# A four-layer convolution net on one core: eight table copies of 64 lags, coefficient arrays loaded once on partition quarters, an unpadded intermediate, and earlier first Toeplitz loads

## The chip, the core and the metric

The kernel runs on one core of a Trainium2 chip, in float32. A core has TensorE (PE; its weight loads are shown as PEld), VectorE (DVE), ScalarE (ACT), GpSimd (POOL) and SyncE (SP), which work side by side, each through its own instructions in order. Transfers between HBM and the on-chip memory run on 16 DMA engines, which SP, ACT and POOL start. The metric is the device time of one execution in microseconds; the median of the runs counts.

## The reference

Four residual layers act on x of shape (8, 56, 56, 192), each behind a group norm. The change lies in layers 0 and 1, which are alike (576 channels inside, Toeplitz products along w and along h):

```python
rpe_input = [0, 1..55, 0, -1..-55]                 # 111 different lags are used
p = silu(x @ p_w.T + p_b)
q = silu(x @ q_w.T + q_b)
v = silu(x @ v_w.T + v_b)
sl = 0.95 + 0.05 * clip(slope, 0, 1)
decay = [1, sl**1..sl**55, 1, sl**55..sl**1]
a1 = mlp1(rpe_input) * decay                       # 1 -> 32 -> 32 -> 32 -> 32 -> 576
a2 = mlp2(rpe_input) * decay
qv = q * v
o1 = toeplitz(qv along w, a1)                      # per channel, 56 x 56
o2 = toeplitz(qv along h, a2)
out = (p * (o1 + o2)) @ o_w.T + o_b
x = x + out
```

Layer 2 is a 7 x 7 depthwise convolution with a two-layer network behind it, layer 3 windowed attention. They are not touched.

## The kernel before, in words

**Statistics.** `input_stats` reads the images in pairs (j = 0 to 3), in seven tiles each, through a buffer of 7 tiles, and takes batch statistics on DVE (L218). They feed the group norm (matmuls at L79).

**q and v.** `tno_qv` works on 2 image pairs at once, in groups of 256 tokens (loads at L240, normalised by ACT at L246), against 1152 columns of `wq` (matmuls L263, added to the bias by DVE at L272). The first two groups are done apart, one image pair at a time (`half_unit`, matmuls L284, additions L291), since only the first pair's statistics are there. ACT applies silu (L301), POOL multiplies q by v (L304), and SP stores the product to HBM as `qv` (L307). There `qv` is [18][64 * 56][128]: 18 blocks of 32 channels by 4 images; a block has 56 image rows of 56 pixels, and 8 rows of padding, which POOL fills with zeros by one transfer for each of the two `qv` arrays (L743).

**Coefficients.** `decay_tables` runs once for each of the two layers. It loads the slopes in five pieces (L145), makes the powers on DVE (L146 to L158), loads the small arrays of each coefficient network (L165 to L174), runs it on PE (L180, L187) and writes the coefficients times the decay (L194) to an HBM table (L204): for each 32 channels 16 rows, row g with the 60 lags from 4g on. Its buffers for the coefficients (`a`) turn over with two.

**Toeplitz.** `tno_toeplitz` walks 9 blocks of 64 channels, for each direction d = 0 (along w) and 1 (along h), 18 steps n in all. Each step loads `q`, 128 partitions of which 2 x 56 are used (d = 0 at L380 by two transfers, d = 1 at L383 by one), and `tm`, the coefficients shifted by one lag per partition, by four transfers (L393); both two steps ahead, through two buffers. PE multiplies (L406), ACT copies out (L413), DVE turns (L424), POOL adds (L429) and stores `L_sum`.

**Order.** `tno_layers` runs the first groups and the statistics by hand, then 28 rounds in which a unit of L263, a statistics tile and one step of each layer's coefficients follow each other, and then four Toeplitz stages, each woven by `weave` into other work of the layers (`tno_qv`, `tno_out`). `weave` counts nominal times that the generators yield; with `lo` the first Toeplitz step is due at 0.04 of the other work. A stage's first yield, after its first loads, counts 8. From the 28 rounds on, PE, DVE, ACT and POOL keep the order written; before them a scheduler places the instructions, as it does SP's throughout. SP's transfers are numbered over eight semaphores, so that each waits for the one eight places before it.

Of the kernel before, what the change touches and what calls it, by code (L numbers as in the profile page):

```python
# [12 lines left out]
F32 = mybir.dt.float32  # L13
# [25 lines left out]
def view(ap, offset, dims):  # L39

    return bass.AP(ap.tensor, ap.offset + offset, [ap.ap[0], *dims])


class Net:
# [86 lines left out]

    TG, TW = 16, 60

    def decay_tables(self, L, p, tables):

        nc, inp = self.nc, self.inp
        tv = p.tile([32, 111], F32, name=f"{L}tv", bufs=1)
        nc.sync.dma_start(tv, inp["tvec"])  # L140
        pows = []
        for c in range(5):
            m = min(128, D1 - 128 * c)
            sl = p.tile([128, 1], F32, name=f"{L}sl")
            nc.sync.dma_start(sl[:m], inp[f"{L}_slope"][128 * c : 128 * c + m, :])  # L145
            nc.vector.tensor_scalar(sl[:m], sl[:m], 0.0, 1.0, ALU.max, ALU.min)  # L146
            nc.vector.tensor_scalar(sl[:m], sl[:m], 1.0 - 0.95, 0.95, ALU.mult, ALU.add)
            pw = p.tile([128, 64], F32, name=f"{L}pw", bufs=5)
            nc.gpsimd.memset(pw[:m, 0:1], 1.0)
            n = 1  # L150
            while n < 64:
                nc.vector.tensor_scalar(
                    pw[:m, n : 2 * n], pw[:m, 0:n], sl[:m], None, ALU.mult
                )
                n *= 2
                if n < 64:
                    sq = p.tile([128, 1], F32, name=f"{L}sl")
                    nc.vector.tensor_mul(sq[:m], sl[:m], sl[:m])  # L158
                    sl = sq
            pows.append(pw)  # L160
            yield 1.0
        for d in range(2):
            t = f"{L}_t{d + 1}"
            w0 = p.tile([32, 2], F32, name="w0")
            nc.sync.dma_start(w0[:, 0:1], inp[f"{t}_w0"])  # L165
            nc.sync.dma_start(w0[:, 1:2], inp[f"{t}_b0"])
            ws = p.tile([32, 3, 32], F32, name="ws")
            nc.sync.dma_start(ws, inp[f"{t}_ws"])
            bs = p.tile([32, 3], F32, name="bs")
            nc.sync.dma_start(bs, inp[f"{t}_bs"])  # L170
            wo = p.tile([32, D1], F32, name="wo")
            nc.sync.dma_start(wo, inp[f"{t}_wo"])
            bo = p.tile([128, 5], F32, name="bo")
            nc.sync.dma_start(bo, inp[f"{t}_bo"])  # L174
            h = p.tile([32, 111], F32, name=f"{L}h")
            nc.vector.tensor_scalar(h, tv, w0[:, 0:1], w0[:, 1:2], ALU.mult, ALU.add)
            nc.vector.tensor_scalar(h, h, 0.0, None, ALU.max)
            for i in range(3):
                hp = self.bank2()[:32, 0, :111]
                nc.tensor.matmul(hp, ws[:, i, :], h, start=True, stop=True)  # L180
                h = p.tile([32, 111], F32, name=f"{L}h")
                nc.vector.tensor_scalar(h, hp, bs[:, i : i + 1], 0.0, ALU.add, ALU.max)
                yield 1.0
            for c in range(5):
                m = min(128, D1 - 128 * c)
                ap = self.bank2()[:, 0, :111]
                nc.tensor.matmul(  # L187
                    ap[:m], wo[:, 128 * c : 128 * c + m], h, start=True, stop=True
                )
                a = p.tile([128, 4 * self.TG + 56], F32, name=f"{L}a")  # L190
                nc.gpsimd.memset(a[:m, 111:], 0.0)
                back = view(pows[c][:m], 55, [[-1, 55]])
                for lo, hi, dec in ((0, 55, back), (55, 111, pows[c][:m, 0:56])):
                    nc.vector.scalar_tensor_tensor(  # L194
                        view(a[:m], 110 - lo, [[-1, hi - lo]]),
                        ap[:m, lo:hi],
                        bo[:m, c : c + 1],
                        dec,
                        ALU.add,
                        ALU.mult,  # L200
                    )
                for n in range(m // 32):
                    to = tables[d][self.TG * (4 * c + n) : self.TG * (4 * c + n + 1)]
                    nc.sync.dma_start(  # L204
                        to.rearrange("g (c w) -> c g w", w=self.TW),
                        view(a[32 * n : 32 * n + 32], 0, [[4, self.TG], [1, self.TW]]),
                    )
                yield 1.0

    def input_stats(self, xs, gn, j, p):  # L210

        nc = self.nc
        st = self.tp.tile([128, 3, 14, 6], F32, name="st", bufs=2)
        for t in range(NT):
            x = p.tile([128, 3, TT], F32, name="x", bufs=7)
            self.load_pair(x, xs, j, slice(t * TT, (t + 1) * TT))
            for k in range(3):
                nc.vector.bn_stats(st[:, k, t, :], x[:, k, :])  # L218
            yield
        self.norms.append(self.pair_gn_finish(st[:, :, :NT], gn, j))  # L220
        for more in self.all_norms():
            pass

    def tno_qv(self, L, j0, xs, gn, qv, apart=None, cols=(0, 2 * D1), g0=0):
# [72 lines left out]
        def multiply(m, n, z, at, c0):  # L297
            k = n // 128
            for f in stores:
                f()  # L300
            nc.scalar.activation(z[:m, :n, :], z[:m, :n, :], AF.Silu)  # L301
            prod = p.tile([128, 4, DC * 4], F32, name="t4")
            half = z[:m, :n, :].rearrange("p (n h c) b -> p n h (c b)", h=2, c=DC)
            nc.gpsimd.tensor_mul(prod[:m, :k], half[:, :, 0], half[:, :, 1])  # L304
            n0 = c0 // 128
            stores[:] = [
                lambda: nc.sync.dma_start(  # L307
                    qv[2 * n0 : 2 * n0 + 2 * k, at : at + m, :].rearrange("n t e -> t n e"),
                    prod[:m, :k].rearrange("p n (h e) -> p (n h) e", h=2),
                )  # L310
            ]
# [53 lines left out]
    def tno_toeplitz(self, j0, mats, qv, o):  # L365
# [6 lines left out]
        def load(n):  # L372
            blk, d = divmod(n, 2)
            q = p.tile([128, H, 128], F32, name="q", bufs=2)
            if d == 0:

                for half in range(2):
                    of = qv[2 * blk + half, :T].rearrange("(h w) e -> w h e", w=W)
                    by = nc.scalar if half and n > 1 else nc.sync
                    by.dma_start(q[64 * half : 64 * half + W], of)  # L380
            else:
                of = qv[2 * blk : 2 * blk + 2].rearrange("n (h w) e -> (n h) (w e)", w=W)
                nc.sync.dma_start(q.rearrange("p i e -> p (i e)"), of)  # L383
            return q

        def matrices(n):

            blk, d = divmod(n, 2)
            row = 32 * self.TW
            at = mats[d].offset + 2 * blk * self.TG * row  # L390
            for k in range(4):
                of = bass.AP(mats[d].tensor, at + k, [[row, 2 * self.TG], [1, row]])
                nc.sync.dma_start(self.tms[n % 2][k:128:4], of)  # L393

        def along(n, q, ot, g):
# [52 lines left out]
        for n in range(2):  # L448
            loaded.append(load(n))
            matrices(n)  # L450
        yield 8.0

        work = []

# [226 lines left out]
    def tno_layers(self, x0, x1, x2, gn, last):  # L681
# [11 lines left out]
        ]  # L693
        qvs = {

            j0: self.dram.tile([D1 // 32, 64 * W, 128], F32, name=f"qv{j0}") for j0 in (0, 2)
        }
        o = [self.dram.tile([B // 2, 9, 128, T], F32, name=f"{L}_sum") for L in LS]
        x = (x0, x1, x2)
        with ExitStack() as ctx, ExitStack() as wqp:  # L700
# [2 lines left out]
            Q = lambda i, j0, *more: self.tno_qv(LS[i], j0, x[i], gn[i], qvs[j0], *more)  # L703
            O = lambda i, j0, woven=True: self.tno_out(LS[i], j0, x[i], gn[i], o[i], x[i + 1], gn[i + 1], woven)
            TZ = lambda i, j0: self.tno_toeplitz(j0, tables[i], qvs[j0], o[i])
            QT, OT, TZT = 25 * 2.25 * 5.3, 28 * 10.7, 8 + 72 * 3.2

            with tc.tile_pool(name="tab", bufs=2) as tab:
                stats = [self.input_stats(x0, gn[0], j, tab) for j in range(4)]
# [1 line left out]
                    pass  # L711
                first, rest = Q(0, 0, tab, (0, 512)), Q(0, 0, None, (512, 2 * D1), 2)
                next(first)

                for n in range(14):
                    next(first)
# [10 lines left out]
                decay = [self.decay_tables(LS[i], tab, tables[i]) for i in range(2)]  # L727
                more = (dt for st in stats[2:] for dt in st)
                with tc.manual_schedule(engines=ENGINES):
                    for n in range(28):  # L730
# [8 lines left out]
                            next(decay[1])  # L739
                        if n in (14, 21):  # L740
                            qv = qvs[0 if n == 14 else 2]
                            to = qv[:, T:].rearrange("n (p k) e -> p n (k e)", p=112)
                            nc.gpsimd.dma_start(to, view(none, 0, [[0, D1 // 32], [1, 512]]))  # L743
                    for more in decay:
                        assert next(more, None) is None
                lanes = [[(rest, QT * 5 / 9 * 21 / 25 - 25.0), (Q(0, 2), QT)], [(O(0, 0), OT), (Q(1, 0), QT)]]
# [4 lines left out]
            with tc.tile_pool(name="tz", bufs=1) as self.tz, in_order:  # L751
# [928 lines left out]
```

## Time and profile before

| What | Value |
| --- | --- |
| Median of 3 runs | 5438.96 us (5432.41 to 5443.45) |
| The profiled execution | 5425.63 us |
| Its span | 5423.8 us |
| PE busy | 5166.0 us (95%) |
| DVE busy | 2589.3 us (48%) |
| ACT busy | 2383.5 us (44%) |
| POOL busy | 1767.2 us (33%) |
| Moved by DMA | 1116.48 MB, mean 206 GB/s |
| Granted TensorE clock, mean | 0.978 |

The span is the time from the first instruction to the last on the core. Busy times overlap, so they do not add up to the span. In the page's rows of 40 slices, each digit is a tenth of busy share in one fortieth of the span (135.6 us).

### The profile page before, as it was taken

To read this page: it belongs to the slowest core of one execution; us is meant where nothing else is said; L and a number is where in the kernel's file an instruction comes from. 1 tells how busy PE (TensorE), PEld (TensorE's weight loads), DVE (VectorE), ACT (ScalarE), POOL (GpSimd) and SP (SyncE) were. 2 spreads that over 40 slices of the span, in tenths; PEclk is the share of its full clock that TensorE was granted. 3 is DMA by queue.
4 is the path that set the end of the run, shared out by engine and by line. 5 is a ranking of instruction groups with operands and counts; after the bars stand their busy time and mean duration, and the time that the engine had idled before them with its cause. 6 is when DMAs were issued, how large, how long until landed. Compare 5 with 4: busy or idle time off the path is not lost.

```text
span 5423.8 us, 144350 instructions
## 1 busy us (share of the span) xinstructions
PE 5166.0 (95%) x64672; PEld 3811.2 (70%) x64672; DVE 2589.3 (48%) x3990; ACT 2383.5 (44%) x3179; POOL 1767.2 (33%) x1291
## 2 busy tenths in 40 slices
PE   7879999999999999999999899989999999999998
PEld 4657777777777777777777789856665444777776
DVE  6535556455555555555556422422222331566666
ACT  3345555444554454655455422243323333444443
POOL 2225675133664243546443100000000100333333
PEclk9889999999999999999999999999999999999998
DMA  7699997888786999889897667635454221445552
GB/s 251 151 243 283 289 311 234 265 281 267 241 262 176 307 317 318 279 226 291 285 312 266 205 223 248 229 96 190 135 174 124 75 68 49 85 98 108 101 102 68
DMA packets 1051146, 1116.48 MB, mean 206 GB/s; under 512 B 235200, under 2 KB 986304, under 8 KB 1036128
## 3 DMA queue, kind: packets, MB, share of 16 engines
q1 hardware_dynamic: 911584, 854.88, 52.9%
q0 software_dynamic: 38144, 200.99, 9.6%
q10 hardware_dynamic: 100800, 51.38, 3.9%
q8 instruction: 508, 8.32, 0.6%
q14 instruction: 110, 0.90, 0.1%
HBM read 743.17 MB, written 363.94 MB: 204 GB/s over the span
## 4 chain that ended last, share of the span: by engine, by line
PE 50%; DVE 3%; DMA 3%; issue 1%; ACT 1%; POOL 1%; SPq 0%; POOLq 0%; ACTq 0%; DVEq 0%
PE bank L980 7%; PE bank L837 5%; PE bank L1060 5%; PE bank L1254 4%; PE bank L263 4%; PE bank L592 3%; PE bank L1074 3%; PE bank L536 3%; PE bank L1370 2%; PE bank L1201 2%; PE bank L1284 2%; PE bank L1325 2%; PE bank L406 2%; PE bank L586 1%; PE bank L1344 1%
## 5 line engine op out<-in xcount | busy, mean ns | idle before, releaser
L263 PE MATMUL bank<-wq,t 128*128 128x256 f32 (+4 forms) x7680 | 1290.3, 374 | 72.1 <-DVE t L272 40.8
L263 PEld LDWEIGHTS bank<-wq,t 128*128 128x128 f32 (+2 forms) x7680 | 1005.2, 190 | 350.8 <-issue 92.4
L272 DVE TENSOR_TENSOR t<-bank,wq 128x1024 f32<-128x1024 f32 (+3 forms) x480 | 517.7, 1112 | 692.5 <-PE bank L263 537.1
L304 POOL TENSOR_TENSOR t<-t 128x1024 f32<-128x1024 f32 (+2 forms) x288 | 528.0, 1847 | 676.5 <-ACT t L301 339.1
L413 ACT COPY ot<-bank 128x896 f32<-128x896 f32 x576 | 493.4, 909 | 515.1 <-PE bank L406 401.8
L429 POOL TENSOR_TENSOR s<-s,ot 128x1568 f32<-128x1568 f32 x128 | 551.1, 4306 | 193.8 <-DVE ot L426 128.4
L301 ACT ACTIVATE t<-t 128x2048 f32<-128x2048 f32 (+2 forms) x288 | 423.0, 1488 | 328.8 <-DVE t L272 319.0
L406 PE MATMUL bank<-q,tm 56*32 56x224 f32 x18432 | 504.9, 353 | 22.0 <-DMA tm<-L_tab 10.6
L406 PEld LDWEIGHTS bank<-q,tm 56*32 56x32 f32 x18432 | 340.0, 106 | 148.2 <-issue 81.7
L122 POOL DMA_DIRECT2D x<-t x112 | 87.0, 777 | 1071.7 <-DVE t L601 1007.4
L560 DVE TENSOR_TENSOR t<-t,bank 128x896 f32<-128x896 f32 x224 | 242.8, 1088 | 401.6 <-ACT bank L555 346.0
L555 ACT ACTIVATE bank<-bank,wo 128x448 f32<-128x448 f32 x448 | 262.8, 605 | 377.4 <-PE bank L545 349.8
L980 PE MATMUL bank<-z,w 128*128 128x448 f32 (+1 forms) x1344 | 413.3, 555 | 2.8 <-DVE xt L828 2.8
L536 PE MATMUL bank<-t,wo 128*128 128x224 f32 x1792 | 375.9, 364 | 21.1 <-ACT t L515 10.6
L536 PEld LDWEIGHTS bank<-t,wo 128*128 128x128 f32 x1792 | 337.7, 194 | 51.7 <-issue 29.6
L592 PE MATMUL bank<-t,wo 128*128 128x224 f32 x1792 | 368.9, 359 | 0.0
L592 PEld LDWEIGHTS bank<-t,wo 128*128 128x128 f32 x1792 | 329.9, 190 | 31.1 <-issue 31.1
L980 PEld LDWEIGHTS bank<-z,w 128*128 128x128 f32 (+1 forms) x1344 | 183.0, 189 | 209.8 <-issue 199.5
L837 PEld LDWEIGHTS bank<-xt,cm 113*112 113x112 f32 x3072 | 309.7, 178 | 25.7 <-issue 23.3
L837 PE MATMUL bank<-xt,cm 113*112 113x108 f32 (+2 forms) x3072 | 316.0, 263 | 1.0 <-ACT h L989 1.0
L127 POOL DMA_DIRECT2D x<-x x64 | 36.7, 573 | 855.5 <-DVE x L1011 796.7
L424 DVE STREAM_TRANSPOSE s<-ot 128x1792 f32<-128x1792 f32 x144 | 292.8, 2034 | 24.5 <-ACT ot L413 16.2
(162 smaller groups left out, 6977.2 us busy)
## 6 DMA issues: line engine op xcount, KB each, us to landing
q<-qv SPq DMA_DIRECT2D x36, 3584.0 KB
t<-L_sum SPq DMA_DIRECT2D x112, 1008.0 KB
L_sum<-s POOLq DMA_DIRECT2D x256, 392.0 KB, 7.2
qv<-t SPq DMA_DIRECT2D x192, 512.0 KB
cm<-in_L_cm SPq DMA_DIRECT2D x96, 896.0 KB
tm<-L_tab SPq DMA_DIRECT2D x288, 240.0 KB
q<-qv SPq DMA_DIRECT2D x40, 1568.0 KB
q<-qv ACTq DMA_DIRECT2D x32, 1568.0 KB
```

The lines of the kernel that those rows point to most:

```text
L263: nc.tensor.matmul(pp[:m, b, 256 * j : 256 * j + k], x[rows, j, 2 if part else b, s : s + m], w[rows, part, c0 + c : c0 + c + k],  start=p ...
L272: nc.vector.tensor_add(z[:m, c : c + k, :], view(pp[:m], 0, [[1, k], [256, 4]]), view(bias[:m], c0 + c, [[1, k], [0, 4]]),)
L301: nc.scalar.activation(z[:m, :n, :], z[:m, :n, :], AF.Silu)
L304: nc.gpsimd.tensor_mul(prod[:m, :k], half[:, :, 0], half[:, :, 1])
L406: nc.tensor.matmul(pt[32 * j : 32 * j + 32, r, hf * 224 : (hf + 1) * 224], tm[rows, at : at + 32], q[rows, :, 4 * c : 4 * c + 4], start=Tr ...
L413: nc.scalar.copy(view(ot, 4 * (g % 4), [[16, 2], [32, 112], [1, 4]]), view(pt, 0, [[512, 2], [4, 112], [1, 4]]),)
L424: nc.vector.transpose(to, of.rearrange("p (i k) -> p i k", k=32))
L429: add.tensor_add(to, to, view(of, 0, [[1, 28], [32, 56]]))
L536: mm(gs[c // 2][:, b, c % 2 * 256 : c % 2 * 256 + N], pw[:, 0, 128 * c : 128 * c + 128], xn[:, b], start=c % 2 == 0, stop=False,)
L592: mm(P[:, b, :N], ow[:, c, 0:128], g[:, 4 * b + c], start=False, stop=c == 3)
L837: nc.tensor.matmul(pc[:, 128 * e + 4 * m0 : 128 * e + 4 * m1], cm[:113, e, k, :], xt[:, m0 - 1 + k : m1 - 1 + k, c + e, :], start=n == 0 a ...
L980: nc.tensor.matmul(phs[c][:, s, :TT], w0[rows, part, at : at + 128], z[rows, Z[2 if part else s], :], start=part == flip, stop=part != flip,)
```

## The change

Five edits come together.

1. The coefficient table keeps 8 rows of 64 lags for each 32 channels, row g with the lags from 8g on, instead of 16 rows of 60. A `tm` transfer reads each row twice, four lags apart.
2. The slopes (two transfers for each layer) and the arrays of all four networks are loaded at the start of `decay_tables`, which is now begun right after the first activation load. The four networks share five arrays, each on a quarter of the partitions. `a` has four buffers, and the statistics' tiles have six instead of seven.
3. `qv` has no padding within blocks: it is [18 * 56 * 56 + 448][128], and only the tail is filled with zeros. The d = 1 load of `q` still reads 64 rows for each half, of which the last 8 are the next block's and not used.
4. A Toeplitz stage's first yield counts 16 instead of 8.
5. In the first stage `lo` is 0.02 instead of 0.04.

The diff, cut to its core:

```diff
-    TG, TW = 16, 60
+    TG, TW = 8, 64
...
+        slopes = p.tile([128, 5], F32, name=f"{L}slopes", bufs=1)
+        nc.sync.dma_start(slopes[:, 0:4], of[:512, 0].rearrange("(c p) -> p c", p=128))
+        nc.sync.dma_start(slopes[:64, 4:5], of[512:D1, :])
+        nets = []
+        for d in range(2):
+            at = slice(64 * (L == "L1") + 32 * d, 64 * (L == "L1") + 32 * d + 32)
...
+            tv, w0, ws, bs, wo = net = [n[at] for n in self.nets]
+            nc.sync.dma_start(w0[:, 0:1], inp[f"{t}_w0"])
+            nc.sync.dma_start(w0[:, 1:2], inp[f"{t}_b0"])
+            nc.sync.dma_start(tv, inp["tvec"])
+            for to, n in ((ws, "ws"), (bs, "bs"), (wo, "wo"), (bo, "bo")):
+                nc.sync.dma_start(to, inp[f"{t}_{n}"])
+        yield 0.0
...
-                a = p.tile([128, 4 * self.TG + 56], F32, name=f"{L}a")
+                a = p.tile([128, 8 * self.TG + 56], F32, name=f"{L}a", bufs=4)
...
-                        view(a[32 * n : 32 * n + 32], 0, [[4, self.TG], [1, self.TW]]),
+                        view(a[32 * n : 32 * n + 32], 0, [[8, self.TG], [1, self.TW]]),
...
-            x = p.tile([128, 3, TT], F32, name="x", bufs=7)
+            x = p.tile([128, 3, TT], F32, name="x", bufs=6)
...
-                    qv[2 * n0 : 2 * n0 + 2 * k, at : at + m, :].rearrange("n t e -> t n e"),
+                    qv[2 * n0 * T : 2 * (n0 + k) * T].rearrange("(n t) e -> t n e", t=T)[at : at + m],
...
-                of = qv[2 * blk : 2 * blk + 2].rearrange("n (h w) e -> (n h) (w e)", w=W)
+                rows = qv.rearrange("(h w) e -> h (w e)", w=W)[2 * H * blk : 2 * H * blk + H + 64]
+                of = bass.AP(rows.tensor, rows.offset, [[H * W * 128, 2], [W * 128, 64], [1, W * 128]])
                 nc.sync.dma_start(q.rearrange("p i e -> p (i e)"), of)
...
-                of = bass.AP(mats[d].tensor, at + k, [[row, 2 * self.TG], [1, row]])
+                of = bass.AP(mats[d].tensor, at + k, [[row, 2 * self.TG], [4, 2], [1, row]])
...
-        yield 8.0
+        yield 16.0
...
-            j0: self.dram.tile([D1 // 32, 64 * W, 128], F32, name=f"qv{j0}") for j0 in (0, 2)
+            j0: self.dram.tile([D1 // 32 * T + 8 * W, 128], F32, name=f"qv{j0}") for j0 in (0, 2)
...
-            QT, OT, TZT = 25 * 2.25 * 5.3, 28 * 10.7, 8 + 72 * 3.2
+            QT, OT, TZT = 25 * 2.25 * 5.3, 28 * 10.7, 16 + 72 * 3.2
...
                 next(first)
+                decay = [self.decay_tables(LS[i], tab, tables[i]) for i in range(2)]
+                for more in decay:
+                    next(more)
...
-                            to = qv[:, T:].rearrange("n (p k) e -> p n (k e)", p=112)
-                            nc.gpsimd.dma_start(to, view(none, 0, [[0, D1 // 32], [1, 512]]))
+                            to = qv[D1 // 32 * T :].rearrange("(p k) e -> p (k e)", p=112)
+                            nc.gpsimd.dma_start(to, none)
...
-                    self.weave(lanes[n], tz, lanes[n + 1][0][0], TZT)
+                    self.weave(lanes[n], tz, lanes[n + 1][0][0], TZT, lo=0.04 if n else 0.02)
```

The matrices, the matmuls and every value computed stay the same.

More of the change, by code (lines that the diff above doesn't have):

```diff
@@ L128, in store_samples @@
             self.nc.gpsimd.dma_start(xs[j + 4 * s, 128:C, tok], of[HALF[s], 2, :])
-    TG, TW = 16, 60
+    TG, TW = 8, 64
     def decay_tables(self, L, p, tables):
         nc, inp = self.nc, self.inp
-        tv = p.tile([32, 111], F32, name=f"{L}tv", bufs=1)
-        nc.sync.dma_start(tv, inp["tvec"])
+        slopes = p.tile([128, 5], F32, name=f"{L}slopes", bufs=1)
+        of = inp[f"{L}_slope"]
+        nc.sync.dma_start(slopes[:, 0:4], of[:512, 0].rearrange("(c p) -> p c", p=128))
+        nc.sync.dma_start(slopes[:64, 4:5], of[512:D1, :])
+        nets = []
+        for d in range(2):
+            t = f"{L}_t{d + 1}"
+            at = slice(64 * (L == "L1") + 32 * d, 64 * (L == "L1") + 32 * d + 32)
+            if at.start == 0:
+                one = lambda n, shape: p.tile([128, *shape], F32, name=f"net{n}", bufs=1)
+                self.nets = one("t", [111]), one("w0", [2]), one("ws", [3, 32]), one("bs", [3]), one("wo", [D1])
+            bo = p.tile([128, 5], F32, name=f"{t}bo", bufs=1)
+            tv, w0, ws, bs, wo = net = [n[at] for n in self.nets]
[4 more added lines that the diff above has]
+                nc.sync.dma_start(to, inp[f"{t}_{n}"])
+            nets.append((at, *net, bo))
+        yield 0.0
         pows = []
@@ L143, in decay_tables @@
             m = min(128, D1 - 128 * c)
-            sl = p.tile([128, 1], F32, name=f"{L}sl")
-            nc.sync.dma_start(sl[:m], inp[f"{L}_slope"][128 * c : 128 * c + m, :])
+            sl = slopes[:, c : c + 1]
             nc.vector.tensor_scalar(sl[:m], sl[:m], 0.0, 1.0, ALU.max, ALU.min)
@@ L162, in decay_tables @@
         for d in range(2):
[L163 to L175, printed above, removed]
+            at, tv, w0, ws, bs, wo, bo = nets[d]
+            h = p.tile([128, 111], F32, name=f"{L}h")[at]
             nc.vector.tensor_scalar(h, tv, w0[:, 0:1], w0[:, 1:2], ALU.mult, ALU.add)
@@ L178, in decay_tables @@
             for i in range(3):
-                hp = self.bank2()[:32, 0, :111]
+                hp = self.bank2()[at, 0, :111]
                 nc.tensor.matmul(hp, ws[:, i, :], h, start=True, stop=True)
-                h = p.tile([32, 111], F32, name=f"{L}h")
+                h = p.tile([128, 111], F32, name=f"{L}h")[at]
                 nc.vector.tensor_scalar(h, hp, bs[:, i : i + 1], 0.0, ALU.add, ALU.max)
@@ L377, in load @@
                 for half in range(2):
-                    of = qv[2 * blk + half, :T].rearrange("(h w) e -> w h e", w=W)
+                    of = qv[(2 * blk + half) * T :][:T].rearrange("(h w) e -> w h e", w=W)
                     by = nc.scalar if half and n > 1 else nc.sync
@@ L726, in tno_layers @@
                         nc.gpsimd.dma_start(t[d][D1 // 32 * self.TG :, :512], none[:1])
-                decay = [self.decay_tables(LS[i], tab, tables[i]) for i in range(2)]
                 more = (dt for st in stats[2:] for dt in st)
```

## The prediction

> **What bounds the kernel now.** I read the page first, then the waits of TensorE (PE) in the first 420 us, then the stretches by stage, then the two tiles that the change touches, and last the trace's DMA packets and semaphore records. From the page:
>
> ```profile
> span 5423.8 us, 144350 instructions
> PE 5166.0 (95%) x64672; PEld 3811.2 (70%) x64672; DVE 2589.3 (48%) x3990; ACT 2383.5 (44%) x3179; POOL 1767.2 (33%) x1291
> PEclk9889999999999999999999999999999999999998
> DMA  7699997888786999889897667635454221445552
> q<-qv SPq DMA_DIRECT2D x36, 3584.0 KB
> ```
>
> PE is busy 95% of the span, so only its idle 258 us, or a resource that becomes slower than PE, can move the end. The DMA row is close to full from slice 3 to slice 20. A third of PE's idle time lies before 420 us; the waits of PE there:
>
> ```profile
> PE bank L79 <- DVE gn_mv L71: 22.4, 3, 19.3
> PE bank L263 <- ACT t L246: 10.8, 1, 10.8
> PE bank L406 <- DMA tm<-L_tab: 10.6, 1, 10.6
> PE bank L180 <- DVE L1h L177: 9.7, 1, 9.7
> PE bank L180 <- issue: 9.7, 2, 7.5
> PE bank L180 <- DVE L0h L177: 8.1, 1, 8.1
> ```
>
> Columns: who waited for whom, us in total, times, longest. These are the waits that the early edits aim at. The four Toeplitz stages, by stretches (busy us of PE, PEld, DVE, ACT, POOL; clock, DMA share, GB/s):
>
> ```profile
> 350.00:930.00 580.00, 542.80 (x7196) 418.70 (x7194) 323.71 (x237) 311.44 (x360) 353.48 (x211) 0.98 0.90 280
> 930.00:1700.00 770.00, 750.86 (x8760) 589.33 (x8756) 416.12 (x436) 375.34 (x513) 327.13 (x206) 0.99 0.79 252
> 1700.00:2310.00 610.00, 593.79 (x7723) 460.66 (x7723) 328.87 (x367) 325.00 (x475) 260.46 (x158) 0.99 0.90 290
> 2310.00:2970.00 660.00, 628.29 (x7998) 489.47 (x7997) 360.91 (x364) 350.32 (x505) 295.48 (x193) 0.98 0.87 279
> 370.00:380.00 10.00, 4.01 (x68) 2.62 (x69) 0.00 (x0) 1.58 (x2) 0.00 (x0) 0.50 1.08 362
> ```
>
> The stages take 2620 us, PE-bound, with the DMA engines 79 to 90% busy: there is little room for a less efficient transfer. The last row holds the first L383 load alone: 16 engines moved 362 GB/s, 22.6 GB/s each. And who waits for these loads today:
>
> ```profile
> L383 SPq DMA_DIRECT2D q<-qv x36: 332/484/11383, 369.2 to 2903.3; - x36
> PE bank L406 <- DMA q<-qv: 3.4, 1, 3.4
> ```
>
> Thirty-six loads of 3584 KB, and PE waited once for one of the q loads, 3.4 us, after 420 us.
>
> **The change part by part.** The sum is made against the profiled execution, 5425.63 us with a span of 5423.8; the median of the three runs is 13.3 us above it, and I carry differences over to the median.
>
> *Coefficient loads moved to the front (32 instead of 36 small ones on SP's queue).* They now stand ahead of the second activation load and of the seven statistics loads of the second image. SP issues such a load every 0.46 us in the trace (45.4 to 48.2 us), and each waits for the one eight before it; the first eight wait behind 7.7 MB of large loads (380 GB/s in the first 20 us) until about 24 us, so the second activation tile is issued near 35 us and lands near 39. PE needs it at 44.7 (the first L284 at 28.4; 22.4 us for eight half units, less 6 for the two that use this tile): covered, with some 4 us to spare. The statistics are not covered. In the built order all 21 now stand on DVE behind six additions of L291, with two additions among them: from 45.2 us, 21 x 0.56 + 2 x 1.2 + 0.7 (aggregate) is 60.1, where PE reached the matmul that needs them at 50.7. Cost +9.6; from 0, if DVE had an earlier slot (its order excludes that), to +15, if the loads land late.
>
> *Slopes there beforehand.* DVE waited 2.1 + 5.3 + 5.5 us for slope loads, in stretches where PE waits for DVE (8.1 and 9.7 at L180, 4.1 at L263): -12.9.
>
> *Twice as many table buffers, half the table bytes* (72 stores: 512 pieces of 240 B become 256 of 256 B). DVE's 4.5 us wait for a table store stands in PE's 7.5 at L180; the 3.2 us of DVE work behind it stays: -4.3.
>
> *Zero fill of 2 x 4032 KB becomes 2 x 224 KB.* The second was issued at 288.3 us and took 18.7 us to land, beside the late activation load that PE's 10.8 us wait ends with: -9.5 (0 to -10.8).
>
> *First q and tm loads one token tile earlier* (7.3 us; the first L406 keeps its place in PE's order): of the 10.6 us wait 3.3 remains, +0.3 for the tables' larger rows: -7.
>
> *Clock.* After such waits 32 matmuls of L263 took 7.3 to 8.5 us instead of 5.65, at a granted clock of 0.5 to 0.76; about 6 us go with the waits. Together: -12.9 - 4.3 - 9.5 - 7 - 6 + 9.6 = -30.
>
> *Eight copies:* 288 tm loads grow by 16 KB: 4.7 MB at 280 GB/s is 17 us of DMA time beside PE; nobody waits, 0 (at most +17). *Later first Toeplitz step in each stage* (16 for 8): the same matmuls slightly denser; 0 (-5 to +10).
>
> *The second q load (L383).* This decides. Before, 128 rows of 28,672 B lie at one step, so the source is [128 rows][7168]. Now the padding rows are gone and the two halves lie 56 image rows apart: the source is [2][64][7168], with 2 as its slowest dimension. The bytes are the same and PE's order around it is the same, so by sizes alone it costs 0. [...]
>
> Price: 3.67 MB on two engines. At the 22.6 GB/s above, 81 us; at the median of the load's own packets in the trace (28,672 B in 1.07 us), 68 us. I take 74, since the other 14 engines will be quiet then. Cover: the load is issued when the block's previous buffer is free, and PE has one half-block, 2620/72 = 36 us, before it needs it. More matters that the two engines also carry their sixteenth of everything else, and SP's later loads and stores queue behind it there, the activation loads and qv stores of the woven lane among them (POOL's multiplies wait for those, and the sums stand behind them). Per engine the stages hold 580 x 0.90 + 770 x 0.79 + 610 x 0.90 + 660 x 0.87 = 2254 us of DMA time; the 36 loads are 132 MB / 362 GB/s = 365 of it, so 1889 is other traffic. On the two engines that becomes 1889 + 36 x 74 = 4553 us. Against 2620 that is +1933. Between stages the loads lie 121, 154 and 119 us apart instead of 50 to 70; there PE works without them and the two engines idle in part. I take 30 us for each gap and for the tail after the last load, +120. The chain alone (74 + 36 = 110 us a block) is shorter than the engines' 4553/36 = 126, so the engines decide.
>
> Sum: -30 + 1933 + 120 = +2023; by sizes alone, without the rule, it would be -30. On the median 5438.96 that is 7462.
>
> **The rivals.** (1) *Serial:* nothing of PE's work hides beside the load, because the lane stops at once. A block then takes 2620/36 + 74 = 147 us: +2664 - 30, about 8070. For it: SP has eight semaphores, and the ninth transfer waits for the load. Against: PE has 36 us of work with data at hand.
> (2) *Cheaper engines:* with 14 engines quiet, packets run at their best, 68 us, and the other traffic takes 10% less: 1700 + 2448 - 2620 = +1528, about 6940.
> (3) *All 16 engines:* the copy is regrouped on its way to the chip and spreads as before. Then only the early edits act, -30: 5409, faster. [...] It decides if the load lands in under 36 us, which takes at least 5 engines.
> (4) As (3), with every unknown at its dear end: the front +15 instead of +9.6, the tm loads +17, the denser steps +10, the late activation load 0 instead of -9.5. That is +12, 5451.
>
> **How the numbers follow.** A change of 0.2% (11 us) is about what a measurement of this kernel can tell from none. Two engines with shared traffic: 0.65, 7462. Serial: 0.16. Cheaper engines: 0.12. All 16: 0.05, of which 0.01 within 0.2%. (4): 0.02. The range takes in (2) and (1), 6900 to 8200, and leaves out (3), (4) and what lies beyond those ends (about 0.1). Faster 0.04, same 0.01, slower 0.95.
>
> **What would show it.** Right: PE's busy share falls to about 70% while its busy time stays; long waits at L413 (the old L406) for "q<-qv" or tm appear, some 36 of tens of us; the DMA share in the stages falls to about half though its bytes stay; the 36 loads lie over 110 us apart. For the early edits: no L146 wait for slopes, a wait near 10 us at L79 for gn_mv at about 50 us, zero fill gone. Wrong: if the load's packets still fill 16 engines for 11 us, the whole sum falls to its first line, -30.

## The result, and the profile after

The changed kernel takes 7665.88 us (median of 4 runs, 7658.03 to 7668.97) where before took 5437.93 us beside it: a ratio of 1.4095, 95% interval 1.407 to 1.412. The prediction was 7462, slower, with a range of 6900 to 8200.

The page of the changed kernel, its first lines and the rows of clock and DMA (40 slices of 191 us; DMA in tenths of the 16 engines):

```profile
span 7656.2 us, 144302 instructions
...
PE 5288.8 (69%) x64672; PEld 3874.4 (51%) x64672; DVE 2592.8 (34%) x3990; ACT 2386.5 (31%) x3179; POOL 1765.2 (23%) x1291
...
PEclk9878677887877887768688677869999999999999
DMA  6545455544535454546455364635673453224443
```

PE has the same 64,672 multiplies and nearly the same busy time (5289 against 5166 us), spread over 2232 us more. Nearly everything is lost in slices 3 to 27; the DMA row there reads 3 to 6 where the same stages had 6 to 9, although the bytes are almost the same (1109 against 1116 MB in all). The transfers got slower while the engines, in the mean, were half idle (a share of 0.45 to 0.54 in the stretches below). The largest waits of PE over the whole span:

```profile
PE bank L413 <- DMA tm<-L_tab: 726.5, 16, 71.7
PE bank L582 <- DVE t L567: 550.0, 20, 62.8
PE bank L413 <- DVE t L278: 265.6, 11, 73.2
PE bank L269 <- DVE t L278: 243.9, 28, 61.3
PE bank L413 <- ACT ot L420: 189.7, 8, 62.9
```

The slow load itself, `q<-qv`, is not among PE's waits, neither here nor in the smaller ones left out. PE waits for the tm loads (ahead of L413), for DVE's multiplies (L567) and bias additions (L278) in the woven lanes, and for ACT's evictions (L420): for what stood behind the slow load. One step further back are GpSimd and VectorE in the same lanes (busy us, mean ns, idle time before them and what ended it), from the trace's groups by line between 350 and 5190 us:

```profile
L310 POOL TENSOR_TENSOR t<-t 128x1024 f32<-128x1024 f32 (+3 forms) x255 | 459.3, 1816 | 1638.9 <-DMA qv<-t 1414.0 <-ACT t L307 194.6 <-ACT ot L420 29.7
...
L567 DVE TENSOR_TENSOR t<-t,bank 128x896 f32<-128x896 f32 x161 | 173.1, 1086 | 1175.0 <-DMA t<-L_sum 720.5 <-ACT bank L562 261.2 <-ACT ot L420 188.9
```

and the same two groups of before, in the same window:

```profile
L304 POOL TENSOR_TENSOR t<-t 128x1024 f32<-128x1024 f32 (+3 forms) x256 | 460.9, 1816 | 515.6 <-DMA qv<-t 290.5 <-ACT t L301 212.0 <-ACT ot L413 12.0
...
L560 DVE TENSOR_TENSOR t<-t,bank 128x896 f32<-128x896 f32 x224 | 242.8, 1088 | 401.6 <-ACT bank L555 346.0 <-DMA t<-L_sum 48.6
```

The multiplies on POOL stood 1414 us behind qv stores instead of 290.5, and the multiplies of the sums on DVE 720.5 us behind loads of L_sum instead of 48.6. Four stretches of the changed kernel (columns as in the prediction: length, busy us of PE, PEld, DVE, ACT, POOL; clock, DMA share, GB/s), the last of them one of the 36 loads:

```profile
350.00:930.00 580.00, 272.87 (x3520) 205.21 (x3520) 146.40 (x111) 151.06 (x180) 165.90 (x97) 0.73 0.45 137
930.00:1700.00 770.00, 454.97 (x5139) 347.73 (x5147) 241.69 (x220) 227.12 (x291) 218.72 (x137) 0.79 0.54 156
...
2970.00:5190.00 2220.00, 1161.52 (x14688) 889.30 (x14675) 641.12 (x670) 617.80 (x889) 527.47 (x330) 0.76 0.51 152
...
488.00:562.00 74.00, 21.81 (x302) 15.66 (x298) 12.04 (x9) 10.51 (x13) 17.90 (x10) 0.68 0.25 91
```

One load takes the 74 us from 488 to 562, in which all 16 engines together move 91 GB/s at a share of 0.25. In before such a load and what ran beside it had 361 GB/s (282 of them the load's own packets) and a share of 1.00:

```profile
437.00:450.00 13.00, 10.63 (x178) 8.33 (x174) 6.93 (x5) 7.87 (x11) 12.69 (x9) 1.00 1.00 361
```

The Toeplitz stages now run from 355 to 5190 us instead of 376 to 2967. The first Toeplitz multiply begins 20.6 us earlier (355.4 against 376.0), so the early edits did move it.

### The profile page after: what moved, and what is told of

Read it like the earlier page. It is cut to its first block, busy times and chain, and to the rows that moved or that the text cites. A ratio compares the mean times of both kernels' runs of the same rounds, so it can differ in the third digit from the quotient of the medians.

```text
span 7656.2 us, 144302 instructions
## 1 busy us (share of the span) xinstructions
PE 5288.8 (69%) x64672; PEld 3874.4 (51%) x64672; DVE 2592.8 (34%) x3990; ACT 2386.5 (31%) x3179; POOL 1765.2 (23%) x1291
## 4 chain that ended last, share of the span: by engine, by line
PE 43%; another core or an unknown queue 26%; DMA 9%; POOL 6%; DVE 5%; issue 5%; SPq 4%; ACT 1%; POOLq 0%; DVEq 0%; ACTq 0%
PE bank L269 7%; PE bank L989 5%; POOL s L436 3%; PE bank L1069 3%; PE bank L1263 3%; PE bank L599 3%; DMA L_sum<-s 3%; DMA qv<-t 3%; PE bank L846 3%; PE bank L543 2%; PE bank L413 2%; POOL t L310 2%; PE bank L1083 2%; PE bank L593 2%
## 5 line engine op out<-in xcount | busy, mean ns | idle before, releaser
L269 PE MATMUL bank<-wq,t 128*128 128x256 f32 (+4 forms) x7680 | 1329.8, 381 | 275.8 <-DVE t L278 243.9
L413 PE MATMUL bank<-q,tm 56*32 56x224 f32 x18432 | 543.8, 373 | 1309.4 <-DMA tm<-L_tab 726.5
L269 PEld LDWEIGHTS bank<-wq,t 128*128 128x128 f32 (+2 forms) x7680 | 1035.8, 195 | 569.9 <-DVE t L278 283.8
L278 DVE TENSOR_TENSOR t<-bank,wq 128x1024 f32<-128x1024 f32 (+3 forms) x480 | 517.1, 1112 | 1708.1 <-POOL t L310 1036.4
L413 PEld LDWEIGHTS bank<-q,tm 56*32 56x32 f32 x18432 | 350.7, 111 | 1457.2 <-issue 556.9
L420 ACT COPY ot<-bank 128x896 f32<-128x896 f32 x576 | 494.9, 908 | 1094.8 <-PE bank L413 716.9
L567 DVE TENSOR_TENSOR t<-t,bank 128x896 f32<-128x896 f32 x224 | 241.2, 1086 | 1335.0 <-DMA t<-L_sum 730.7
L582 PE MATMUL bank<-t,wo 64*64 64x224 f32 x448 | 75.1, 406 | 557.2 <-DVE t L567 550.0
L582 PEld LDWEIGHTS bank<-t,wo 64*64 64x64 f32 x448 | 24.4, 140 | 592.7 <-DVE t L567 579.9
```

What stands on the lines that cost most here:

```text
L269: nc.tensor.matmul(pp[:m, b, 256 * j : 256 * j + k], x[rows, j, 2 if part else b, s : s + m], w[rows, part, c0 + c : c0 + c + k],  start=p ...
L278: nc.vector.tensor_add(z[:m, c : c + k, :], view(pp[:m], 0, [[1, k], [256, 4]]), view(bias[:m], c0 + c, [[1, k], [0, 4]]),)
L413: nc.tensor.matmul(pt[32 * j : 32 * j + 32, r, hf * 224 : (hf + 1) * 224], tm[rows, at : at + 32], q[rows, :, 4 * c : 4 * c + 4], start=Tr ...
L420: nc.scalar.copy(view(ot, 4 * (g % 4), [[16, 2], [32, 112], [1, 4]]), view(pt, 0, [[512, 2], [4, 112], [1, 4]]),)
```

## The experiments

Kernels made from before keep its line numbers (L406, L263, L560); in those made from the changed kernel some stand one line earlier (L412 is its L413). All rows of the table were counted from the DMA packets of each kernel's trace, between the first packet of the first second-q load and the last packet of the last one ("period"). A packet of this load is one row, 28,672 B. *k* is the number of engines on which the author's account puts the load. It was an assumption, which the recorded texts call a rule; no record names the engine of a packet. What the packets show is how many of them are in flight at once: most often 2 in the changed kernel (83% of the time in which any is) and with 122 rows (over 80%), 4 with 124 rows, 11 with 121 and 16 with the single transfer of before (46%). In the mean, by packet time times rows over the load's time, they are 12.9 in before, 12.6 with even and odd rows, 12.9 and 11.9 with the halves, 12.8 with the third part undone, 1.8 in the changed kernel and with 122 rows, and 1.75 with the load on ACT's queue. In this sense "a load on k engines" stands below for k packets in flight. "Load" is the load's packet time over k, "other" that of the other packets over all 16 engines; "share" is their sum over the period.

| kernel | k | packet mean (median), us | one load, us | load + other per engine, us | period, us | share | median us, ratio [95%] |
|---|---|---|---|---|---|---|---|
| before | 16 | 1.21 (1.07) | 12.0 | 349 + 1853 | 2546 | 0.865 | 1 |
| even / odd rows | 16 | 1.21 (1.07) | 12.3 | 349 + 1856 | 2552 | 0.864 | 5439.28, 1.0007 [0.9997, 1.0016] |
| two halves | 16 | 2.03 (2.13) | 20.1 | 585 + 1969 | 2845 | 0.898 | 5722.29, 1.0514 [1.0500, 1.0529] |
| halves on two queues | 16 | 2.03 (2.07) | 21.8 | 585 + 1968 | 2816 | 0.907 | 5685.11, 1.0461 [1.0445, 1.0476] |
| 121 rows | 11 | 1.93 (1.96) | 25.8 | 764 + 1973 | 2993 | 0.915 | 5877.76, 1.0805 [1.0790, 1.0821] |
| 124 rows | 4 | 1.61 (1.57) | 61.5 | 1802 + 2087 | 4154 | 0.936 | 7029.26, 1.2917 [1.2899, 1.2935] |
| 122 rows | 2 | 1.10 (1.06) | 75.6 | 2416 + 2025 | 4603 | 0.965 | 7472.28, 1.3734 [1.3708, 1.3760] |
| after | 2 | 1.12 (1.06) | 79.4 | 2570 + 2082 | 4799 | 0.969 | 7665.88, 1.4095 [1.4070, 1.4119] |
| load on ACT's queue | 2 | 1.13 (1.06) | 82.6 | 2604 + 2128 | 4877 | 0.970 | 7699.03, one run |
| third part undone | 16 | 1.20 (1.07) | 12.0 | 346 + 1925 | 2597 | 0.874 | 5460.95, 1.0045 [1.0028, 1.0062] |

**122 rows instead of 128, in the kernel before.** One number changes, the layout and the single-step address stay:

```diff
-                nc.sync.dma_start(q.rearrange("p i e -> p (i e)"), of)
+                nc.sync.dma_start(q.rearrange("p i e -> p (i e)")[:122], of[:122])
```

> The kernel before, with one number changed: its second q load takes 122 rows instead of 128 (the multiplies read 120). [...] Theory: other traffic 1889 us per engine, and 36 x 74 x 122/128 = 2539: 4428 us against 2620, and 120 for the gaps, so about +1930: 7365 us, or near 7560 if it loses what the changed kernel lost in its stages. Rival (the two-part address, not the number of engines, is what costs): within 10 us of before, since it moves 5% fewer bytes.

Measured 7472.28 us, +2032 on before, with 5% fewer bytes in that load. Its long waits are those of the changed kernel:

```profile
PE bank L406 <- DMA tm<-L_tab: 660.9, 16, 56.4
PE bank L263 <- DVE t L272: 392.6, 30, 56.6
PE bank L575 <- DVE t L560: 349.7, 19, 59.1
```

So the padding, the tables, the arrays and the two-part address are not needed to lose 2000 us. 122 rows, with 2 packets in flight instead of 16, do it alone.

**124 rows, the same edit with 124.**

> [...] It tells the engine's share of all traffic from the load's own time. Engines decide: a load takes 74 x 2/4 x 124/128 = 36 us on each of four engines, 1889 + 36 x 36 = 3180 us against 2620: about +560, 6000 us (up to 6120 with gaps between loads). The load's own time decides (the lane waits only for what exceeds its 36 us of cover): 36 us are covered, 5440 to 5500 us.

Measured 7029.26 us, +1589: not the load's own time, which says at most 5500, and also 900 us more than the engines' account had. The load's stretch from 492 to 552 us shows what was mis-sized:

```profile
492.00:552.00 60.00, 27.16 (x381) 20.32 (x379) 11.90 (x9) 15.29 (x20) 21.80 (x14) 0.74 0.44 137
```

Sixty us instead of 36, because the packets took 1.61 us, not the 1.06 of the two-engine load. With the measured packets the account comes near: 1802 + 2087 is 0.936 of the period.

**121 rows, the same edit with 121.**

> The same with 121 rows, 11 engines by the rule: 74 x 2/11 x 121/128 = 12.7 us a load, 1889 + 36 x 12.7 = 2347 us on each of the eleven engines, less than PE's 2620. Engines decide: no change, 5430 to 5450 us. A rival in which any departure from 16 engines costs in proportion to its engines (a load 1.4 times as long, on PE's path): 36 x 3 = +100 us, 5540.

Measured 5877.76 us, +437. Both expectations missed. Packets took 1.93 us and a load 25.8 us where 12.7 were expected. That is still inside the 36 us of cover, and it still cost 437 us: cover doesn't decide. With the measured packets each of the eleven engines had 764 + 1973 = 2737 us of work, more than the 2546 us that the same loads took in before.

**Two transfers of 64 rows, one for each half, in the changed kernel.**

```diff
-                of = bass.AP(rows.tensor, rows.offset, [[H * W * 128, 2], [W * 128, 64], [1, W * 128]])
-                nc.sync.dma_start(q.rearrange("p i e -> p (i e)"), of)
+                to = q.rearrange("p i e -> p (i e)")
+                for half in range(2):
+                    at = rows.offset + half * H * W * 128
+                    nc.sync.dma_start(to[64 * half : 64 * half + 64], bass.AP(rows.tensor, at, [[W * 128, 64], [1, W * 128]]))
```

> The changed kernel, with the second q load of a block written as two transfers of 64 rows, one for each half, so that the slowest dimension of both sides is 64 instead of 2 on the source. Everything else of the change stays. Theory (the load's two engines are the whole loss): about 5409 us, the early edits' -30 against before, or 5417 by the -20.6 us that the first Toeplitz multiply moved in the trace of after; L413's waits for tm fall from 727 us to under 20. Rival (the loss comes from the rest of the change: unpadded rows, table rows of 64, coefficient arrays): above 7000 us.

Measured 5722.29 us, 5.1% above before. It gets back 1944 of the 2228 us, which clears the rest of the change of most of the loss; but the forecast of 5409 fell. From 442 to 458 us, one load (1792 KB twice):

```profile
442.00:458.00 16.00, 15.08 (x261) 10.59 (x258) 9.04 (x7) 8.86 (x13) 15.69 (x10) 1.00 0.99 223
```

The engines are 99% busy and move 223 GB/s, the other traffic included, where the window of before had 361. Each packet takes 2.13 us in the median, twice the 1.06.

**Even and odd rows, in the kernel before.** Again two transfers of 64 rows on 16 engines, but each over all 128 partitions:

```diff
+                to = q.rearrange("p i e -> p (i e)")
+                for odd in range(2):
+                    nc.sync.dma_start(to[odd::2], of[odd::2])
```

> The kernel before, with the second q load of a block written as two transfers of 64 rows, one for the even and one for the odd rows, each reaching over all 128 partitions. As many transfers, rows and bytes as in the 64-row halves of the changed kernel, whose packets took 2.1 us instead of 1.06. [...] Rival (two transfers instead of one cost it, whichever rows they take): packets of 2.1 us, loads of 17 to 20 us, about 5720.

Measured 5439.28 us, no difference, where the author's theory had 5440 to 5560 and the rival about 5720, and packets of 1.07 us:

```profile
441.00:454.00 13.00, 10.59 (x169) 8.28 (x170) 6.92 (x5) 7.59 (x10) 12.69 (x9) 0.87 1.01 373
```

Two transfers of 64 rows cost nothing by themselves (ratio 1.0007). What is left is which 64 rows one transfer takes: in the halves they go to one half of the partitions, and they also come from one contiguous half of the source. No run changes the partitions and leaves the source rows as they were, so which of the two makes the packets take 2.13 us is not shown.

**The second half from ACT's queue.**

```diff
+                    by = nc.scalar if half and n > 1 else nc.sync
+                    by.dma_start(to[64 * half : 64 * half + 64], ...)
```

> The kernel with the two 64-row halves, with the second half issued from ACT's queue instead of SP's, so that both run at once, as the first q loads of a block do already. [...] Rival (16 engines with four rows each are slow as such): 5720, whatever the queue.

Measured 5685.11 us, nearer to the rival's 5720 than to the 5450 to 5560 that the author had for halves that run at once: by the ratios (1.0461 against 1.0514) 29 us came back. Of the 32 blocks whose halves come from two queues, 15 have them overlap by more than 3 us (1140 to 1157 and 1142 to 1158 us, say); in the others one half ran after the other. But where they overlap, packets take 1.8 to 2.1 us too. No record here shows which rows an engine moves when, so the cause stays open. That 64 rows in one transfer are slow as such, the rival's reason, does not agree with the even and odd rows and their packets of 1.07 us.

**The two-engine load issued by ACT.**

```diff
-                nc.sync.dma_start(q.rearrange("p i e -> p (i e)"), of)
+                nc.scalar.dma_start(q.rearrange("p i e -> p (i e)"), of)
```

> The changed kernel with the two-engine load issued by ACT instead of SP. Theory (the two engines that carry the load are the bound, whoever issues it): 7500 to 7800 us, the same loads of 70 to 80 us, 118 to 150 us apart. Rival (SP's queue is the bound: its later loads and stores stand behind this one on its rings and semaphores, and ACT's few would not): below 6900 us.

One run: 7699.03 us, loads of 82.6 us. It is a single run, but the rival's 6900 us is far off: SP's queue is not the bound. What the three slowest kernels have in common is the two engines (1.75 to 1.8 packets in flight in the mean).

**The third part undone: padding rows and the 128-row load are back, the rest of the change stays.**

```diff
-                rows = qv.rearrange("(h w) e -> h (w e)", w=W)[2 * H * blk : 2 * H * blk + H + 64]
-                of = bass.AP(rows.tensor, rows.offset, [[H * W * 128, 2], [W * 128, 64], [1, W * 128]])
+                of = qv[2 * blk : 2 * blk + 2].rearrange("n (h w) e -> (n h) (w e)", w=W)
...
-                            to = qv[D1 // 32 * T :].rearrange("(p k) e -> p (k e)", p=112)
-                            nc.gpsimd.dma_start(to, none)
+                            to = qv[:, T:].rearrange("n (p k) e -> p n (k e)", p=112)
+                            nc.gpsimd.dma_start(to, view(none, 0, [[0, D1 // 32], [1, 512]]))
```

> The changed kernel with its third part alone undone: qv has its padding rows again, so the second q load is one transfer of 128 rows at one step, as before, and the zero fill is 2 x 4032 KB again. The coefficient arrays at the front, the eight copies of 64 lags, the table buffers and the later first step stay. Theory (the whole loss sits in that load): packets of 28,672 B back at 1.06 us median, a load in 10 to 12 us, and the early edits without the smaller zero fill: the first Toeplitz multiply moved by 20.6 us in the changed kernel, less the 9.5 us that I gave to the zero fill: about -11 on before, 5430 (from 5418 to 5440). Rival (the rest of the change costs the 282 us that the two 64-row transfers left): about 5720.

Measured 5460.95 us, ratio 1.0045 [1.0028, 1.0062]. The load is repaired (packets 1.07 us median), and of the two halves' 282 us some 255 (1.0514 against 1.0045) were the load's own. But the sign is wrong: the first Toeplitz multiply begins at 362.8 us, 13 us before that of the kernel before, and the end is 24 us later. The early gain was lost inside the stages, so the next three runs take the rest apart.

**Coefficient loads behind the statistics.** `next(more)` of both `decay` moves from ahead of the loop to after its seventh statistics load.

> The kernel with the third part undone, and in it the coefficient arrays' loads moved behind the seven statistics loads of the second image. Theory (these loads made the statistics late, 8.5 us of PE's waiting at L79 in the changed kernel): L79's wait for gn_mv falls below 2 us, the first Toeplitz multiply moves up by about as much, and the time by 5 to 9 us against the same kernel without this step. Rival (the time moves into the next wait, for the slopes at L152 or the late activation load at L246): the first Toeplitz multiply within 2 us of where it was.

Early waits of PE, first with the third part undone:

```profile
PE bank L412 <- DVE t L278: 14.2, 1, 14.2
PE bank L79 <- DVE gn_mv L71: 11.9, 3, 8.5
...
PE bank L269 <- ACT t L252: 7.9, 3, 6.6
```

and with the loads moved back:

```profile
PE bank L79 <- DVE gn_mv L71: 23.1, 3, 19.7
PE bank L412 <- DVE t L278: 15.2, 1, 15.2
PE bank L269 <- ACT t L252: 10.8, 4, 5.5
```

The 19.7 us is the first wait of the kernel, 19.0 in the other and put down there to the weights' load; without it L79 waits 3.4 us instead of 11.9, where below 2 was expected. The first multiply moves by 3.8 us, to 359.0, since the activation wait at L269 takes 2.9 us of it and others the rest. The time, 5454.48 us and 1.0035 [1.0022, 1.0047], lies 6 us lower with intervals that overlap: the wait is shown, the gain in time is not.

**Sixteen copies of 60 lags again.**

```diff
-    TG, TW = 8, 64
+    TG, TW = 16, 60
...
-                of = bass.AP(mats[d].tensor, at + k, [[row, 2 * self.TG], [4, 2], [1, row]])
+                of = bass.AP(mats[d].tensor, at + k, [[row, 2 * self.TG], [1, row]])
```

> The kernel with the third part undone and the coefficient loads behind the statistics, and in it sixteen copies of 60 lags again instead of eight of 64 (288 tm loads of 240 KB, each row read once). Theory (the tm loads are what is left of the loss: their packets of 8192 B took 361 to 374 us median in ns, 410 mean, where the 7680 B of before took 291 and 329, which is 47 us of every engine's time in stages that are 82 to 91% DMA): packets back at 291, stages shorter by 40 to 50 us, 5405 to 5415, faster than before by 20 to 30. Rival (the later first step and the earlier start of the first stage pack the work worse, and the tables cost the 17 us at most that I gave them): 5437 to 5450.

Measured 5442.03 us, 1.0026 [1.0016, 1.0037]: not the 5405 to 5415 of the theory. The tm packets came back (7680 B, 291 ns median) and took 191 instead of 234 us of each engine in the loads' period; the loads' period fell by 21 us, from 2596 to 2575. But the first multiply started 9.5 us later (368.5): with sixteen copies PE's longest wait for the late activation load at L269 is 15.2 us instead of 5.5 (the table stores beside it are twice as large again; that they cause it is inferred). In the sum 5 us by the ratios and 12 by the medians of two chips, with overlapping intervals.

**The later first step undone too.**

```diff
-        yield 16.0
+        yield 8.0
...
-            QT, OT, TZT = 25 * 2.25 * 5.3, 28 * 10.7, 16 + 72 * 3.2
+            QT, OT, TZT = 25 * 2.25 * 5.3, 28 * 10.7, 8 + 72 * 3.2
...
-                    self.weave(lanes[n], tz, lanes[n + 1][0][0], TZT, lo=0.04 if n else 0.02)
+                    self.weave(lanes[n], tz, lanes[n + 1][0][0], TZT)
```

> The same with the later first step undone as well (8 instead of 16 per stage, the first stage's share of the lane as before). What is left of the change are the coefficient arrays in one go, the slopes with them and four table buffers. Theory (the later steps are worth nothing, from -5 to +10 by the prediction): within 8 us of the kernel with sixteen copies. Rival (they are what the loss of 24 us was): 20 us or more below it.

Measured 5425.49 us, 0.9995 [0.9988, 1.0001], on the same chip as the 5442.03: 16.5 us, with intervals apart. The idle time of PE ahead of the Toeplitz multiplies, with the later steps (columns: ns, shortest, median and longest; first and last start in us; below, us and times):

```profile
L412 PE MATMUL bank<-q,tm x18432: 346/349/579, 368.5 to 2985.9; 56*32 56x224 f32 x199
...
  DVE t L278: 16.7, 4
  ACT ot L419: 15.2, 9
```

and with the old ones:

```profile
L412 PE MATMUL bank<-q,tm x18432: 349/349/579, 371.4 to 2964.8; 56*32 56x224 f32 x199
...
  DVE t L278: 2.8, 4
...
  ACT ot L419: 2.1, 2
```

The multiplies start 2.9 us later and end 21.1 us sooner. With the changed weave PE ran into evictions by ACT and bias additions on DVE that weren't done, 27 us more of waits. The two steps and the share `lo` were undone together; which of them does it stays open.

**The zero fills earlier.** What is left of the change (arrays in one go, slopes, four table buffers) makes no difference by itself, because PE waits 16.8 us at L269 for an activation load that a zero fill of 4032 KB at 280 us runs beside:

```diff
-                        if n in (14, 21):
-                            qv = qvs[0 if n == 14 else 2]
+                        if n in (3, 11):
+                            qv = qvs[0 if n == 3 else 2]
```

> The kernel with coefficient loads behind the statistics, sixteen copies and the old steps, and in it the two zero fills of 4032 KB issued at the fourth and the twelfth step of the joint loop instead of the fifteenth and the twenty-second (near 147 and 207 us by the trace, where the DMA engines are 43 to 54% busy, instead of 228 and 280). Theory (the fill makes the activation load late that PE waits 16.8 us for at L269; that wait fell to 1.1 us where the fill was 224 KB): the wait under 5 us, the first Toeplitz multiply near 359 instead of 371.4, and the time 10 to 14 us below the same kernel: about 5413, 0.2 to 0.3% below before. Rival (the time moves into the first tm load, which stands at 11.7 us already): first multiply within 4 us of 371, time within 5 us of 5425.

Waits before, with the fill at 280 us:

```profile
PE bank L269 <- ACT t L252: 22.1, 4, 16.8
PE bank L412 <- DMA tm<-L_tab: 11.7, 1, 11.7
```

and with it earlier:

```profile
PE bank L412 <- DMA tm<-L_tab: 11.3, 1, 11.3
...
PE bank L269 <- ACT t L252: 4.2, 2, 4.0
```

Its Toeplitz multiplies, by the trace's rows of that line:

```profile
L412 PE MATMUL bank<-q,tm x18432: 346/349/579, 352.1 to 2940.2; 56*32 56x224 f32 x199
```

Measured 5415.40 us against 5435.73, 0.9958 [0.9944, 0.9972]: 0.4% faster than before, and the only version that is clear of noise below it. Against the same kernel without this step that is 10 us by the medians and 20 by the ratios, on two chips (10 to 14 expected). The first multiply starts 19.3 us earlier (352.1), more than the 12.8 us by which the longest wait shrank, and the tm wait did not grow.

## Why the prediction was right

*Two engines.* Right. That a source of 2 x 64 rows would put the load on two engines, the first term of the price, was an assumption that no run of before shows; in its place the changed kernel shows two packets of the load in flight for 83% of its time. 122 rows lost 2032 us without any other edit, and moving the load to ACT's queue changed little. Of the signs named, PE's share of 69%, the DMA shares of 0.45 to 0.54 and loads 135 us apart came; of 36 waits at L413 for q or tm only 16 did, all for tm (726.5 us); the rest of the delay reached PE through POOL, DVE and ACT.

*Size of the engines' account.* The prediction had 1889 + 36 x 74 = 4553 us per engine, plus 120 of gaps. Measured are 2082 + 2570 = 4652, which leaves 147 us of the period of 4799. Two terms were off in opposite ways, so that the sum came nearer than its parts, which is luck: the load's packets took 71 us of an engine (1.115 x 64) instead of 74, -94; the other traffic came out 193 us above the 1889. (In before it measures 1853: the load that was priced at 362 GB/s did not run alone there, its own packets made 241 of them.) Its packets were nearly the same in number and longer: those of 512 B took 36 ns in the mean where they took 33, which is 92 us, and the larger tm packets made 62 us more. The third difference is the base: I set the sum against 2620 us of stages, while the loads' own period was 2546. That is 74 us, and with +99 for the engines and +27 for the gaps it makes 200 of the 204 us by which the forecast was short.

*Serial (8070).* Fell: lanes went on beside the load (PE worked 21.8 of its 74 us), and the waits lie in many places.

*Cheaper engines (6940).* Half of it was so, the load's packets ran at their best in the median (1.064 us, 68 us for 64); but the other traffic became dearer, not 10% cheaper, and this sum left out the 120 us of gaps.

*All 16 engines (5409).* Did not happen, and its threshold was wrong. I wrote that a load under 36 us, or 5 engines, would be hidden. A load of 20.1 us cost some 255 us and one of 25.8 us cost 437. In before the engines' packets already filled 0.865 of the period, and the two halves, with 283 us more per engine than the kernel with the third part undone (2554 against 2271), made the period 248 us longer. That the engines were a second bound beside PE is how I read these figures; no run takes the two apart. "There is little room" was the right reading and should have gone into the rival.

*Early edits (-30).* The first Toeplitz multiply moved by -20.6. PE's waits in the changed kernel's first 420 us, to be read against those in the prediction:

```profile
PE bank L79 <- DVE gn_mv L71: 11.9, 3, 8.5
PE bank L186 <- issue: 9.0, 3, 4.3
PE bank L413 <- DMA tm<-L_tab: 7.9, 1, 7.9
...
PE bank L186 <- DVE L1h L183: 4.6, 1, 4.6
...
PE bank L269 <- ACT t L252: 1.3, 2, 1.1
```

The late statistics cost 8.5 us at L79 (+9.6 forecast, 9.4 by its own figures); the waits of the coefficient networks fell from 27.5 (L180) to 13.6 us (L186), against -12.9 and -4.3 forecast for slopes and table buffers; the late activation wait fell from 10.8 to 1.1 us (-9.5 forecast); the first tm load was still waited for 7.9 us (3.3 forecast). With the 128-row load back, nothing of this start reached the end: the later first step and `lo`, set at 0 with +10 at most, cost 16.5 us, and the eight copies, set at 0 and +17 at most, 5 to 12 us and 43 us of engine time where I had 17. With the padding rows and the 128-row load the change (which then has the large zero fill again) was 24 us slower, beyond the rival (4) with all its dear ends (+12). So the -30 was wrong in sign for the whole, and the forecast was not hurt by it because the load outweighs it by far.

## What to carry to other kernels

Before a load's address is rewritten, look at how its rows are laid out and divided: here 128 rows at one step had 16 packets in flight most often, of 1.07 us each in the median; two halves of 64 rows had 12.9 in the mean, of 2.13 us; and a source of 2 x 64 rows, or 122 rows at one step, had two, of 1.06 us. Judge a transfer by the packet time that it puts on the engines it uses, against the time the stage has for them, not by whether its own latency is covered: a load of 25.8 us under 36 us of cover cost 437 us here. When a start moves earlier and the end doesn't, look for what the weave gives back inside the stages, and undo the schedule's edits one by one.

## What the runs showed of the hardware that was not expected

A 28,672 B packet of this load took 1.06 to 1.07 us (27 GB/s) where a transfer of 128 rows had 16 of them in flight and where a load had two, in the changed kernel and with 122 rows; but 2.13 us in the halves, 1.96 us with 121 rows and eleven in flight, and 1.57 us with 124 rows and four in flight (medians). The halves differ from the even and odd rows, whose packets took 1.07 us, in the partitions and in the source rows that one transfer takes, and no run separates these. Which rows an engine moves is on no record here, so the slow packets of the halves, of 121 and of 124 rows stay unexplained.
